# Row scatters of a routed two-expert layer: three supertiles at each end leave at once

## The chip, the cores and the metric

The kernel runs on one core of a Trainium2 chip. The metric is device time in microseconds of one execution. A core has five engines that run side by side and wait for each other by semaphores: TensorE (PE, with its weight loads as PEld), VectorE (DVE), ScalarE (ACT), GpSimd (POOL) and SyncE (SP). Each has its own instruction stream, which it executes in order. Transfers are issued by SyncE (plain ones here) and by GpSimd (indirect ones), and run on 16 shared DMA engines.

## The reference

The input x has 32 sequences of 256 tokens of 128 numbers, 8192 tokens in all. Two residual steps follow each other, both with a layer norm whose scale and shift come from a small conditioning matrix:

```python
h = _layernorm(x) * (1 + ca) + sa
x = x + ga * attn(h)       # g, a = sigmoid(linear(h)); v = linear(h)
                           # s_t = a_t * s_{t-1} + (1 - a_t) * v_t along the sequence; s * g
h = _layernorm(x) * (1 + cb) + sb
x = x + gb * ffn(h)

# ffn: 8 experts, each token goes to its best two
logits = x_flat @ gate_w.T + gate_b
probs = softmax(logits)
topk_vals, topk_idx = top_k(probs, 2)
h = relu(x_flat @ w1[e] + b1[e])     # 128 -> 512
y = h @ w2[e] + b2[e]                # 512 -> 128
out = sum over the two experts of topk_val * y
```

All arithmetic is float32; the up-projection is computed with the operands split into a leading part and a rest.

## The kernel before, in words

**The front.** Tokens are cut into 16 supertiles of 512 (`ST`; `T` = 4 tiles of 128). Each goes through four steps: the first norm (`a_norm`), the gates and the scan (`a_mix`), the residual and second norm (`a_res`), and the routing (`a_route`). `HEAD` and the list `steps` run them as a pipeline: step t works on several supertiles at once, each at another stage.

**The rows on their way out.** `a_route` writes, for each of a supertile's 4 tiles and 2 choices, 128 rows of 130 numbers (the normed token, its weight and its place in the output) into a tile `rw`, of which there are three, and computes the row numbers `pi` at which they belong in an expert-sorted region `reg` in HBM. The eight indirect transfers (L447) that scatter them are not issued there: L453 puts them on a list, `sending`. The function `drip` takes a few from it: one or two after each step of the front (L725), and one, later two, in each turn of the expert part (L648). Each then waits, by a dependence added by hand (L465), for a given ScalarE instruction of that step, so that it leaves at that pace. `sent` keeps what was issued.

**The tables.** After some supertiles (`TAKE`) a table says which blocks of 256 rows of `reg` are complete, and of which expert they are. There are 71 blocks. The first table, after supertile 2, has 5; after supertile 12 the tables together have 45 (blocks 0 to 44); the last one, after supertile 15, has the other 26. A table's blocks wait in `held` and are moved to `blocks` when its supertile's eight scatters have been issued (L467 to L469).

**The expert part.** `b_step` runs one turn: it issues loads for up to `LOOK` blocks ahead (`b_load`, L538 and L544: the rows `xr`, 130 KB, and the expert's first weights `ww`, 514 KB), transposes one block (`b_in`, L551 to L554), does the up-projection of the one before (`b_up`, L566 to L574), and the down-projection of the one before that (`b_down`, L584 to L591), whose result `yt` goes by two indirect transfers (L593) to `yd` in HBM. There are eight `yt` tiles and five `ww` tiles. The load of a block waits, by hand again (L540), for the last 16 row scatters in `sent`, that is, for the last two supertiles' rows issued before it in the order of the program. `between` puts such turns between the steps of the front; after the last step (`alive = False`) the turns run alone. At the end `c_load` and `c_add` read both results of each token, add them and write the output.

**Who sets the order.** The order in which instructions are written is not the order in which they are built: a scheduler that models the engines' times orders each engine's stream, with the front at a higher priority (`AHEAD`). On GpSimd the row scatters (L447), the block outputs (L593) and the small copies into `rw` (L445) share one stream. A copy of the normed rows into `rw` (L402, ScalarE) has to wait until the scatters that read this tile three supertiles earlier have landed.

Of the kernel before, what the change touches and what calls it, by code (L numbers as in the profile page):

```python
# [16 lines left out]
WAIT = mybir.DependencyInfo(mybir.DependencyClass.Sync, mybir.DependencyReason.DATA)  # L17
# [7 lines left out]
T = 4  # L25
BLK = 256

TAKE = (2, 3, 4, 5, 6, 7, 8, 10, 12)
CUT = 9

HEAD = "n0|m0 n1|r0 m1 n2|R0 r1 m2 n3|R1 r2 m3 n4|R2 r3 m4 n5"

# [22 lines left out]
def adaln_moe(ctx: ExitStack, tc: tile.TileContext, x, Wg, bg, Wv, bv, Wd, bd,  # L55
# [7 lines left out]
    NS = N // ST  # L63
    BPS = ST // S
    JB = T // BPS
    K = 2
# [5 lines left out]
    of = out.rearrange("b s d -> (b s) d")  # L72
# [19 lines left out]
    rows = cp.tile([P, D], F32, name="rows")  # L92
# [38 lines left out]
    def full(s):  # L131
        return max(0, -((E * (BLK - 1) - K * (s + 1) * ST) // BLK))

    def touched(s):
        return (K * (s + 1) * ST + E * (BLK - 1)) // BLK


    CLS = [CUT] + list(range(TAKE[-1], NS))
    NC = len(CLS)
# [80 lines left out]
    def late_constants():  # L220
        nc.vector.tensor_copy(b2s[:, 0], b2r)
        nc.vector.tensor_tensor(b2s[:, 1], b2r, b2s[:, 0], op=ALU.subtract)
        for h in range(2):
            nc.sync.dma_start(b2w[h:h + 1].bitcast(F32), b2s[:, h].bitcast(F32))


        sT3 = cp.tile([P, 3, NB], F32, name="sT3")
        nc.vector.tensor_copy(sT3, sT.unsqueeze(1).to_broadcast([P, 3, NB]))
        pr = psa.tile([P, 512], F32, tag="pq", name="pr")
        nc.tensor.matmul(pr[:N3, :D], sT3.rearrange("p a b -> p (a b)"), wm[:, 5 * D:], start=True, stop=True)  # L230
        mr = cp.tile([N3, D], F32, name="mr")
        guarded(mr, pr[:N3, :D], [N3, D], 1.0, "gr")
        nc.vector.tensor_copy(mr3, mr)
        for i in (1, 2, 2):
            w = slice(i * NB, (i + 1) * NB)
            nc.vector.tensor_tensor(mr[w], mr[w], mr3[w], op=ALU.subtract)
            nc.vector.tensor_copy(mr3[w], mr[w])

        nc.vector.tensor_tensor(sel, ident[:N3, 0:NB], ident[:N3, NB:2 * NB], op=ALU.add)
        nc.vector.tensor_tensor(sel, sel, ident[:N3, 2 * NB:N3], op=ALU.add)  # L240

    def stage(e):
        w1s = bk.tile([P, H], F32, tag="hh", name=f"w1s{e}")
        nc.sync.dma_start(w1s, w1[e])
        wh = bk.tile([P, WW], F32, tag="ww", name=f"wh{e}", bufs=5)
        nc.scalar.activation(wh[:, :H].bitcast(F32R), w1s, AF.Copy)
        nc.gpsimd.tensor_tensor(wh[:, H:2 * H].bitcast(F32R), w1s, wh[:, :H], op=ALU.subtract)
        nc.gpsimd.tensor_copy(wh[:, O_B1:], cols[:, 3 + e * NH:3 + (e + 1) * NH])
        nc.sync.dma_start(wd[e], wh)
# [62 lines left out]
    def a_norm(s):  # L312
        g = LN1G.get(s, 0)
        if g:
            mv = wk.tile([P, g * T, 2], F32, tag=f"mva{g}", name=f"mva{s}")
            for i in range(g):
                stats(mv[:, i * T:(i + 1) * T], xa[:, s + i], f"a{s + i}")
            y, r = rsqrt(mv, f"a{s}", s)
            for i in range(g):
                ln1[s + i] = (y[:, i * T:(i + 1) * T], r[:, i * T:(i + 1) * T])  # L320
        y, r = ln1[s]
        xn = wk.tile([P, T, D], F32, tag="xn", name=f"xn{s}")
        for j in range(T):
            last = nc.scalar.activation(xn[:, j], xa[:, s, j], AF.Identity, scale=y[:, j], bias=r[:, j])  # L324
        return dict(s=s, xn=xn, last=last)
# [43 lines left out]
    def a_res(a):  # L369
        s, og = a["s"], a["og"]  # L370
        xt = xa[:, s]
        po = early(s, "pbx", f"po{s}")
        for j in range(T):
            nc.tensor.transpose(po[:, j * P:(j + 1) * P], og[:, j * P:(j + 1) * P], ident)
        xm = xt.rearrange("p t d -> p (t d)")
        nc.vector.tensor_tensor(xm, po, xm, op=ALU.add)
        mv = wk.tile([P, T, 2], F32, tag="mvb", name=f"mvb{s}")
        stats(mv, xt, f"b{s}")
        y, r = rsqrt(mv, f"b{s}", s)
        xn = wk.tile([P, T, D], F32, tag="xm", name=f"xm{s}")  # L380
        for j in range(T):
            a["last"] = nc.scalar.activation(xn[:, j], xt[:, j], AF.Identity, scale=y[:, j], bias=r[:, j])
        a["xn"] = xn

    def a_route(a, base):
        s, xn = a["s"], a["xn"]
# [64 lines left out]
            return w.ins  # L451

        sending.extend((s, send, j, k) for j in range(T) for k in range(K))  # L453
        return rk[:, T]


    sending = []
    sent = []
    held = []

    def drip(n, behind):
        for _ in range(min(n, len(sending))):
            s, send, j, k = sending.pop(0)
            w = send(j, k)
            tc.add_manual_dep(w, behind.ins.name, WAIT, reason="pace of the rows on their way out")  # L465
            sent.append(w)
            if not sending or sending[0][0] != s:  # L467
                while held and held[0][0] <= s:
                    blocks.extend(held.pop(0)[1])  # L469

    def table(i, counts, done, n, last):

# [49 lines left out]
    def fills(base):  # L522
        fi = wk.tile([1, E], I32, tag="fi", name="fi")
        nc.vector.tensor_copy(fi, base[0:1, :])
        for e in range(E):
            r = nc.sync.value_load(fi[0:1, e:e + 1], min_val=e * CAP, max_val=e * CAP + N)
            w = nc.sync.dma_start(reg[bass.ds(r, BLK)].rearrange("(t p) d -> p t d", p=P), pad)
            into_reg(w.ins, "fill")
# [97 lines left out]
    blocks = []  # L626
# [33 lines left out]
    def between():  # L660
        nonlocal slot
        slot += 1
        if slot % SKIP and len(blocks) - len(flow) > BACK:
            b_step()

    counts = []
    st = {}

    def late():

        for s in range(XE, NS):
            load_x(s)
        for e in range(E):
            nc.sync.dma_start(wr[:, e].rearrange("p (k o) -> p k o", o=D), w2[e].rearrange("(k p) o -> p k o", p=P))


    steps = [[("nmrR".index(w[0]), int(w[1:])) for w in part.split()] for part in HEAD.split("|")]
# [6 lines left out]
    for t, todo in enumerate(steps):  # L684
        def step3(s):
            nonlocal base, done
            with tc.high_priority(AHEAD[3] * (s >= EARLY)):
                base = a_route(st[s], base)
                if s in CLS:
                    b = cp.tile([P, E], F32, name=f"cnt{s}")  # L690
                    nc.vector.tensor_copy(b, base)
                    base = b
                    counts.append(b)
                nb = len(blocks) + sum(len(x) for _, x in held)
                if s in TAKE:
                    n = full(s) - nb
                    tb, done = table(s, counts[:1] * (s > CUT) + [base], done, n, False)
                    held.append((s, [(tb, q, []) for q in range(n)]))
                elif s == NS - 1:
                    n = touched(s) - nb  # L700
                    tb, done = table(NS, counts, done, n, True)
                    fills(base)
                    rest = [(tb, q, []) for q in range(n)]
                    held.append((s, rest))
                    z = 0
                    for c in CLS:
                        u = max(E, touched(c) - nb) if c == CUT else touched(c) - nb
                        rest[u - 1][2].extend(range(z, c + 1))
                        z = c + 1

        def step2(s):
            with tc.high_priority(AHEAD[2] * (s >= EARLY)):
                a_res(st[s])

        def step1(s):
            with tc.high_priority(AHEAD[1] * (s >= EARLY)):
                a_mix(st[s])

        def step0(s):
            with tc.high_priority(AHEAD[0] * (s >= EARLY)):  # L720
                st[s] = a_norm(s)

        for i, s in todo:
            (step0, step1, step2, step3)[i](s)
            drip(2 if t < len(steps) - NS or len(sending) > K * T else 1, st[s]["last"])  # L725
            between()
        if t == 0:
            for e in range(E):
                stage(e)
            late()  # L730
        if t == LATE:
            late_constants()
# [32 lines left out]
```

## Time and profile before

The median of three runs is 546.61 us (538.9 to 547.15). The profiled execution took 472.67 us, 470.9 of it the span between the first and the last instruction.

| | busy us | share of the span | instructions |
|---|---|---|---|
| PE | 411.4 | 87% | 2810 |
| PEld | 346.6 | 74% | 2810 |
| DVE | 283.6 | 60% | 1511 |
| ACT | 291.4 | 62% | 726 |
| POOL | 291.9 | 62% | 322 |

The mean granted clock of TensorE was 0.908. 91.52 MB were moved, at 194 GB/s on average.

A group of the profile reads: line, engine, operation, what is written from what, count, then busy time and the mean of one in ns, then the idle time of the engine just before these instructions and what ended most of it. "issue" is time in which the engine waited for nothing that the profile shows. A line of the timeline reads: start, length (both in us), engine, line, operation, and in brackets the idle time before it with what released it. SPq lines are transfers that SyncE issues; their length is that of the issue.

### The profile page before, as it was taken

How to read it: one execution, taken by the hardware profiler on the slowest of the kernel's cores; microseconds unless marked ns; L12 is line 12 of the kernel's file. 1: busy time of each engine (PE TensorE's matmuls, PEld its weight loads, DVE VectorE, ACT ScalarE, POOL GpSimd, SP SyncE). 2: the span in 40 equal slices, each digit the busy share in tenths (PEclk: the TensorE clock that was granted, in tenths of full speed). 3: DMA queues.
4: the chain of work that ended last, by engine and by line, in shares of the span. 5: the costliest groups of instructions: out<-in, count | busy, mean ns of one | idle time of the engine just before them, and what ended most of it. 6: DMA issues, size and time to landing. Idle time of an engine off the chain costs nothing.

```text
span 470.9 us, 11399 instructions
## 1 busy us (share of the span) xinstructions
PE 411.4 (87%) x2810; PEld 346.6 (74%) x2810; DVE 283.6 (60%) x1511; ACT 291.4 (62%) x726; POOL 291.9 (62%) x322
## 2 busy tenths in 40 slices
PE   4867767779999999998997999999949999899980
PEld 3324433458888888987886999999839999799970
DVE  6899999958987886883795535222102214344564
ACT  4777563777978778774665565555415566656540
POOL 3634655536777777777577777777773444534551
PEclk9895666679999999997999799999979999999996
DMA  6996211192727566455452766686269979999983
GB/s 198 335 314 248 91 34 40 42 284 92 239 77 253 149 191 184 146 156 162 154 163 62 228 199 192 187 275 173 89 183 285 282 210 278 303 327 314 279 244 113
DMA packets 81845, 91.52 MB, mean 194 GB/s; under 512 B 8577, under 2 KB 66408, under 8 KB 81782
## 3 DMA queue, kind: packets, MB, share of 16 engines
q1 hardware_dynamic: 73024, 73.84, 53.6%
q0 software_dynamic: 8704, 16.94, 10.4%
q8 instruction: 26, 0.43, 0.4%
q14 instruction: 37, 0.30, 0.2%
q10 hardware_dynamic: 54, 0.02, 0.0%
HBM read 64.24 MB, written 27.43 MB: 195 GB/s over the span
## 4 chain that ended last, share of the span: by engine, by line
PE 65%; DMA 10%; DVE 9%; ACT 7%; issue 4%; POOL 3%; SPq 2%; POOLq 0%; ACTq 0%; DVEq 0%
PE pby L587 26%; PE p L566 7%; PE pz L346 6%; PE p L567 6%; PE p L568 6%; PE pby L584 4%; PE pbx L551 3%; DMA reg<-rw,pi 2%; DMA yd<-yt,xr 2%; DMA xa<-in_L_attn_x_dram 2%; DMA ww<-wd 2%; DMA yk<-yd 2%; PE pl L397 2%; PE px L337 2%; POOL yd L593 1%
## 5 line engine op out<-in xcount | busy, mean ns | idle before, releaser
L593 POOL DMA_INDIRECT yd<-yt,xr x142 | 142.5, 1004 | 87.2 <-ACT yt L591 49.5
L447 POOL DMA_INDIRECT reg<-rw,pi x128 | 124.8, 975 | 52.5 <-issue 21.1
L587 PE MATMUL pby<-wr,hh 128*128 x1136 | 151.5, 286 | 0.0
L587 PEld LDWEIGHTS pby<-wr,hh 128*128 128x128 f32 x1136 | 137.2, 196 | 9.4 <-issue 0.9
L574 ACT ACTIVATE hh<-p,ww 128x256 f32<-128x256 f32 x231 | 97.6, 475 | 20.0 <-PE p L568 14.1
L591 ACT ACTIVATE yt<-pby,xr 128x128 f32<-128x128 f32 x142 | 44.9, 364 | 80.6 <-PE pby L587 80.6
L566 PE MATMUL p<-xs,ww 128*128 128x256 f32 x284 | 89.5, 317 | 4.6 <-DMA ww<-wd 4.0
L554 DVE TENSOR_TENSOR xs<-pbx,xs 128x256 fp32r<-128x256 f32 x71 | 29.9, 421 | 86.7 <-ACT xs L553 86.5
L568 PE MATMUL p<-xs,ww 128*128 128x256 f32 x284 | 81.6, 288 | 0.0
L567 PE MATMUL p<-xs,ww 128*128 128x256 f32 x284 | 81.5, 287 | 0.0
L346 PE MATMUL pz<-h,wT 128*128 128x512 f32 x96 | 58.8, 734 | 6.1 <-ACT tg L361 3.6
L566 PEld LDWEIGHTS p<-xs,ww 128*128 128x128 f32 x284 | 55.2, 195 | 6.3 <-issue 3.1
L567 PEld LDWEIGHTS p<-xs,ww 128*128 128x128 f32 x284 | 55.5, 195 | 0.7 <-issue 0.7
L568 PEld LDWEIGHTS p<-xs,ww 128*128 128x128 f32 x284 | 55.1, 194 | 0.2 <-issue 0.2
L346 PEld LDWEIGHTS pz<-h,wT 128*128 128x128 f32 x96 | 19.7, 233 | 21.6 <-issue 9.4
L551 PE MATMUL pbx<-ident,xr 128*128 128x128 f32 x142 | 28.8, 286 | 6.0 <-DMA xr<-reg 6.0
L572 DVE TENSOR_SCALAR hh<-p,ww 128x256 f32<-128x256 f32 x53 | 25.4, 480 | 12.4 <-ACT hh L574 10.3
L553 ACT ACTIVATE xs<-pbx 128x256 fp32r<-128x256 f32 x71 | 27.5, 387 | 7.4 <-PE pbx L551 7.4
L324 ACT ACTIVATE xn<-xa,nra,nya 128x128 f32<-128x128 f32 x64 | 26.4, 488 | 8.0 <-DVE nra L307 8.0
L618 DVE TENSOR_TENSOR ot<-yk 128x512 f32<-128x512 f32 (+1 forms) x17 | 11.3, 663 | 32.7 <-DMA yk<-yd 17.7
L584 PE MATMUL pby<-b2w,ones_r 2*128 x71 | 27.2, 383 | 2.3 <-ACT yt L591 2.0
L402 ACT ACTIVATE rw<-pb 128x1024 f32<-128x1024 f32 x16 | 16.3, 1022 | 18.4 <-issue 6.2
(181 smaller groups left out, 594.7 us busy)
## 6 DMA issues: line engine op xcount, KB each, us to landing
ww<-wd SPq DMA_DIRECT2D x71, 514.0 KB
xr<-reg SPq DMA_DIRECT2D x71, 130.0 KB
yk<-yd SPq DMA_DIRECT2D x30, 256.0 KB
wd<-wh SPq DMA_DIRECT2D x8, 514.0 KB
xa<-in_L_attn_x_dram SPq DMA_DIRECT2D x16, 256.0 KB
out_dram<-ot SPq DMA_DIRECT2D x15, 256.0 KB
yd<-yt,xr POOLq DMA_INDIRECT x142
w1s<-in_L_ffn_w_dram SPq DMA_DIRECT2D x8, 256.0 KB
```

Source lines behind the costliest of these rows:

```text
L346: nc.tensor.matmul(z, wT[:, i], h1, start=True, stop=True)
L447: w = nc.gpsimd.indirect_dma_start(out=reg, out_offset=bass.IndirectOffsetOnAxis(ap=pi[:, j * K + k:j * K + k + 1], axis=0), in_=rw[:, j, ...
L551: nc.tensor.transpose(px[:, j * P:(j + 1) * P], xr[:, j, 0:D], ident)
L554: nc.vector.tensor_tensor(xs[:, 1], px, xs[:, 0], op=ALU.subtract)
L566: nc.tensor.matmul(z, hi, xs[:, 0], start=True, stop=False)
L567: nc.tensor.matmul(z, hi, xs[:, 1], start=False, stop=False)
L568: nc.tensor.matmul(z, lo, xs[:, 0], start=False, stop=True)
L574: w = nc.scalar.activation(hh[:, k], p1[:, k - k0], AF.Relu, bias=bias)
L584: nc.tensor.matmul(py.rearrange("p (j d) -> p j d", d=D), ones_r, b2t, start=True, stop=False)
L587: nc.tensor.matmul(py[:, j * D:(j + 1) * D], hh[:, k, j * P:(j + 1) * P], we[:, k * D:(k + 1) * D], start=False, stop=(j == NJ - 1 and k = ...
L591: nc.scalar.activation(yt[:, j], py[:, j * D:(j + 1) * D], AF.Copy, scale=xr[:, j, D:D + 1])
L593: w = nc.gpsimd.indirect_dma_start(out=yd, out_offset=bass.IndirectOffsetOnAxis(ap=xr[:, j, D + 1:D + 2].bitcast(I32), axis=0), in_=yt[:, ...
```

## The change

Supertiles outside a range `PACED` = (3, 13), that is 0, 1, 2 and 13, 14, 15, issue their eight scatters at the end of `a_route`, together with all that is still on the list, and without the wait for a ScalarE instruction. Those of supertiles 3 to 12 stay on the list. The release of a table's blocks becomes a function, which is called after each scatter and also once at the end of the routing step. In the step loop the condition on the first three steps is dropped.

```diff
+PACED = (3, 13)
...
         sending.extend((s, send, j, k) for j in range(T) for k in range(K))
+        if not PACED[0] <= s < PACED[1]:
+            drip(len(sending), None)
         return rk[:, T]
...
+    def release():
+        while held and not (sending and sending[0][0] <= held[0][0]):
+            blocks.extend(held.pop(0)[1])
 
     def drip(n, behind):
         for _ in range(min(n, len(sending))):
             s, send, j, k = sending.pop(0)
             w = send(j, k)
-            tc.add_manual_dep(w, behind.ins.name, WAIT, reason="pace of the rows on their way out")
+            if behind:
+                tc.add_manual_dep(w, behind.ins.name, WAIT, reason="pace of the rows on their way out")
             sent.append(w)
-            if not sending or sending[0][0] != s:
-                while held and held[0][0] <= s:
-                    blocks.extend(held.pop(0)[1])
+            release()
...
                         rest[u - 1][2].extend(range(z, c + 1))
                         z = c + 1
+                release()
...
-            drip(2 if t < len(steps) - NS or len(sending) > K * T else 1, st[s]["last"])
+            drip(2 if len(sending) > K * T else 1, st[s]["last"])
```

## The prediction

> **What bounds the kernel now.** I read the slices first, then the two GpSimd groups, then the timeline where the slices dip, then busy times by stretch. The rows of the slices are tenths of busy time in slices of 11.8 us.
>
> ```profile
> PE   4867767779999999998997999999949999899980
> POOL 3634655536777777777577777777773444534551
> PEclk9895666679999999997999799999979999999996
> ...
> L593 POOL DMA_INDIRECT yd<-yt,xr x142 | 142.5, 1004 | 87.2 <-ACT yt L591 49.5
> L447 POOL DMA_INDIRECT reg<-rw,pi x128 | 124.8, 975 | 52.5 <-issue 21.1
> ```
>
> TensorE is full from 106 us on, except for two slices (247 to 259 us, a 7; 341 to 353 us, a 4). GpSimd at 7 looks free but is not: each scatter takes 0.98 us and then shows 0.30 us of "issue", so a scatter costs 1.27 us of the queue, and tenths of 7 to 8 mean a queue that never rests. The timeline of GpSimd shows starts 1.27 us apart almost without a break from 111 to 353 us. So two engines are full at once between 111 and 345 us. The hole comes from the second:
>
> ```profile
> 327.14 0.37 SPq L538 DMA_DIRECT2D xr<-reg  x1
> 331.13 0.38 PE L551 MATMUL pbx<-ident,xr 128*128 128x128 f32 x2
> ...
> 338.71 0.99 POOL L593 DMA_INDIRECT yd<-yt,xr  x1 [0.30 <-DMA reg<-rw,pi]
> ...
> 341.29 0.97 POOL L447 DMA_INDIRECT reg<-rw,pi  x1 [0.30 <-DMA yd<-yt,xr]
> 342.56 0.95 POOL L447 DMA_INDIRECT reg<-rw,pi  x1 [0.30 <-DMA yd<-yt,xr]
> 343.82 0.98 POOL L593 DMA_INDIRECT yd<-yt,xr  x1 [0.30 <-DMA reg<-rw,pi]
> 344.96 0.37 SPq L538 DMA_DIRECT2D xr<-reg  x1
> 345.64 0.35 SPq L544 DMA_DIRECT2D ww<-wd  x1
> 347.20 0.48 PE L551 MATMUL pbx<-ident,xr 128*128 128x128 f32 x1 [4.10 <-DMA xr<-reg]
> ```
>
> The last row scatter (L447, supertile 15) starts at 342.56; block 45 of 71, the first of the last table, waits for it and is loaded at 344.96, 2.40 us later. Bias matmuls of successive blocks (L584) start 3.93 us apart before and after: 328.93, 332.86 ... 362.50, 366.44. Blocks 42 and 47 stand at 332.86 and 362.50; five intervals are 19.65 us, so the hole costs 10.0 us. The stretches, with columns window, length, busy PE, PEld, DVE, ACT, POOL, clock, DMA share, GB/s:
>
> ```profile
> 60.00:82.00 22.00, 15.92 (x48) 8.20 (x46) 20.90 (x142) 11.77 (x26) 12.71 (x14) 0.66 0.12 40
> 82.00:98.00 16.00, 10.83 (x41) 6.91 (x41) 14.70 (x133) 11.13 (x24) 8.31 (x9) 0.61 0.31 82
> 98.00:106.00 8.00, 6.94 (x39) 5.77 (x40) 4.18 (x33) 6.23 (x15) 1.92 (x2) 0.79 0.97 319
> ...
> 335.00:355.00 20.00, 12.48 (x80) 11.15 (x79) 1.82 (x4) 5.15 (x14) 14.48 (x15) 0.83 0.50 152
> ```
>
> Before 98 us VectorE is the full engine (35.6 of 38 us from 60 to 98) and TensorE idles 12.3 us between 60 and 106.
>
> **What the Trainium skill says.** "DMA: Bandwidth & Descriptors", section "Anatomy of one DMA — SWDGE (gpsimd) path", puts the fixed cost of such a DMA at about 2.0 us, mostly the receipt of the write, and has semaphore waits done by the issuing sequencer before dispatch. The trace agrees: a row scatter lands 2.27 us after its start (chain of waits, 337.45), while the next starts after 1.27. So eight scatters in a row cost 8 x 1.27 = 10.2 us of queue, and a waiting scatter holds all behind it. The same page, "Issuing engines are not separate DMA queues", says that all issuers share the 16 DMA engines; here that hardly matters: GpSimd's queue takes 10.4% of them. "TensorE: Matmul & The Clock Gate", section "What's actually happening", has the array slow until it has been kept busy; the clock is 0.66 from 60 to 82 us and 1.00 from 106 to 180.
>
> **The change part by part.** The sum is made against the profiled execution: 470.9 us of span plus 1.8 around it, 472.67. The median of the runs shown, 546.61, is 73.9 us longer; no view shows where. If it is TensorE that runs slower there, GpSimd has slack and the hole shrinks. So I carry both: the profile as it stands, and a run paced by TensorE.
>
> *Start.* The first table's five blocks wait for the 24 row scatters of supertiles 0 to 2. Now the last of these starts at 89.86 and block 0 is loaded at 92.46. In the changed program they stand back to back after one copy. Supertile 0 ends as before; the 16 others start at 60.0, so the last starts at 60.0 + 15 x 1.265 = 79.0, and block 0's load leaves at about 81.6, 11 us earlier. On TensorE the block now stands ahead of a transpose of the front that ran at 82.87, and its up-projection ahead of supertile 5's; its weights landed 4.7 us after issue (93.65 to 98.3), so they come at about 87.5. Front work waits some 5 us there, ScalarE and VectorE with it. Three blocks (11.8 us) are done before the front's step at 103.81; at most 6.3 us of idle lie after 82, and a warmer clock gives perhaps 2 more. TensorE thus gains 6 to 8 us; the front gets 4 to 6 us later. GpSimd gains less: by 110.7 us it has done 33 of these DMAs, afterwards some 36, since it must wait for block 0's output around 100 us: 3 x 1.27 = 4 us (0 to 7).
>
> *Middle.* Supertiles 3 to 12 keep their pace: the edit of the count in the step loop touches the first three steps alone, in which no row is ready yet, so it costs 0. Three extra blocks lie ahead of each front step. The rings of three rw tiles stay tied to GpSimd: ScalarE already waits there (4.7 us at 252). Cost: 0 in the sum, -3 to +4 us for the range.
>
> *End.* Supertiles 13, 14 and 15 lose eight waits each. This costs no engine anything; it moves queue positions. In the built order the outputs of blocks 35 to 40, 12 scatters, go behind supertile 15's rows instead of ahead: -12 x 1.28 = -15.4 us. Last row scatter: 342.56 - 15.4 = 327.2, minus the 4 us of the start = 323.2; the waiting load follows 2.40 later, at 325.6.
>
> But SyncE's loads wait for the last 16 scatters *written before them in the program*. Before, supertile 15's were written a few at a time between the loads of blocks 40 to 45, so only block 45 needed the last. Now all are written at once, and in the built order it is block 40's load that waits on all eight queue lanes. Blocks 40 to 44 belong to an older table and need none of these rows. So 31 blocks, not 26, come after the wait. The old rest took 470.9 - 344.96 = 125.9 us; five blocks more make 125.9 + 19.65 = 145.6. The end is 325.6 + 145.6 = 471.2: **+0.3 us**. The break-even is a load at 325.3. The stall itself moves from block 45 to block 40 and does not get smaller: TensorE, three blocks ahead, runs dry near 315. What is late next is again supertile 15's last scatter, with four block outputs (31 to 34) ahead of it. Block outputs now wait up to 20-odd us on GpSimd; the ring of eight yt tiles (eight blocks, 31 us) covers that, and if it did not, ScalarE would stall within the hole.
>
> *If TensorE paces the run*, GpSimd's 1.27 us a scatter hides behind blocks of about 5 us (3.93 x 546.61/472.67 = 4.5, more where only TensorE slows), neither hole opens, and what remains is the start: -6 to -8 us.
>
> Between 0 and -7 I take -4 us: **543 us**.
>
> **The rivals.**
> *The wait goes away (about 531).* If GpSimd keeps up, supertile 15's rows leave when its indices are ready (pi at 291.85) plus 10.2 us and no load is late: 10.0 us of hole and 6 to 8 of start, 16 to 18 us, 529 to 531. For: dense 1.27 us spacing can vanish when TensorE is slower. Against: 12 scatters saved out of 210, and outputs 31 to 34 stand ahead; and if GpSimd keeps up because TensorE is slow, there was less hole to win.
> *Slower (about 558).* Mechanism: the waiting load moved to block 40 with a queue that is not ahead. The bursts of supertiles 13 and 14 push the last two rows of supertile 12 behind eight others (10.2 us); rw of supertile 15 needs that buffer, ScalarE waits for it in order, and the block outputs ahead of supertile 15's rows come late. Every microsecond of the load after 325.3 is one lost; from 336 on it is over 2%. For: this wait already took 4.7 us at 252 and 1.4 at 290. Against: by the count of the queue that row moves by five DMAs (6 us) less the 4 of the start. With 12 us of it: 558.
> *It does not do what it says.* The waits are gone from the built program, so no.
> *Nothing measurable.* The profile case alone: 547.
>
> **How the numbers follow.** Forecast, the stall moves and little changes (539 to 549): 0.62. The wait goes: 0.24. Slower: 0.14. Two per cent (10.9 us) is about what a measurement of this kernel can tell from no change; its three runs lie 8 us apart. Of the 0.24 some 0.18 is beyond 535.7, of the 0.14 some 0.11 beyond 557.5; the forecast's own edges add 0.01 each. Range: 531 to 555, which takes in the first rival's upper half and the start of the second; it leaves out about 0.2.
>
> **What would show it.** In the profile after: block 0 loaded near 82 us and TensorE fuller from 84 to 106; row scatters of supertiles 13 to 15 in three groups of eight, 1.27 us apart; the gap in row loads ahead of block 40, ending near 326; a PE slice that dips near 315 to 335; 31 blocks at 3.93 us after it. Wrong would be: a load of block 40 before 315 or after 336; no gap at all; waits of ScalarE on row scatters beyond 10 us; a TensorE that idles as long before 106 us as now. The total goes wrong if the 74 us between profile and median sit elsewhere than in TensorE, since then their share in each stage is unknown.

## The result and the profile after

The changed kernel took 562.1 us (median of 4, 559.12 to 565.02) against 544.62 for the kernel before: a ratio of 1.036 (95% interval 1.024 to 1.047), slower. 543 us was forecast, with a range of 531 to 555.

One and the same program ran, by whole series of runs, at one of two levels, and one chip gave both: the kernel before at 474.5 to 475.7 us (here called the lower level, three series and the profile before) or at 543.0 to 546.8 us (the upper level, five series, among them the timed comparison and the profile after), so that only a comparison within a level tells what the change does.

The slices and the two GpSimd groups of the kernel after (span 560.9 us, so slices of 14.0 us):

```profile
PE   5658606987689799886978974775769999989991
POOL 4537650366376666646566565736343454534452
PEclk9976657979689899899889796878689999999996
...
L600 POOL DMA_INDIRECT yd<-yt,xr x142 | 142.1, 1001 | 140.9 <-ACT yt L598 110.3
L449 POOL DMA_INDIRECT reg<-rw,pi x128 | 123.8, 967 | 90.8 <-issue 35.4
```

GpSimd is no longer a full queue: it waits 110.3 us for results of blocks, where it waited 49.5. Only from 420 us on is TensorE full for more than two slices on end. It dips at 56 to 84 us, where the 24 scatters of supertiles 0 to 2 leave, and from 322 to 420 us, where those of 13 to 15 leave. The stretches at the start, with columns window, length, busy PE, PEld, DVE, ACT, POOL, clock, DMA share, GB/s:

```profile
60.00:82.00 22.00, 8.27 (x24) 4.11 (x22) 9.09 (x71) 8.76 (x20) 15.57 (x17) 0.58 0.15 48
82.00:98.00 16.00, 10.28 (x41) 6.58 (x42) 15.12 (x104) 7.20 (x15) 0.00 (x0) 0.71 0.69 207
98.00:106.00 8.00, 8.00 (x55) 6.83 (x55) 7.57 (x62) 6.37 (x16) 0.85 (x1) 0.90 0.01 3
```

The scatters do leave back to back (17 GpSimd instructions in 22 us), and block 0 is loaded at 82.24 us. But VectorE, the full engine of this stretch, is busy for 9.09 us where it was 20.90. Its timeline shows how:

```profile
69.59 0.17 DVE L522 TENSOR_SCALAR g<-g 128x8 f32<-128x8 f32 x1 [0.42 <-DVE smt L516]
70.33 0.16 DVE L305 SCALAR_TENSOR_TENSOR nya<-nta,nya 128x4 f32<-128x4 f32 x1 [0.57 <-DVE g L522]
71.74 0.15 DVE L517 TENSOR_SCALAR tb<-smt 128x1 int32<-128x1 f32 x1 [1.25 <-DVE nya L305]
...
75.98 0.17 DVE L524 TENSOR_TENSOR done<-g,done 128x8 f32<-128x8 f32 x1 [1.88 <-remote]
```

Small operations of 0.15 us stand 0.4 to 1.9 us behind VectorE's own last instruction, or behind nothing that the profile can name ("remote"). The profile before has no such line between 66 and 84 us. The profile after is of the upper level and the profile before of the lower one, so these differences hold what the level does as well as what the change does; in the paced kernel at the upper level (e16 below) VectorE is busy for 18.33 us of this stretch.

The end, in the timeline of GpSimd, TensorE and SyncE's loads:

```profile
391.90 0.96 POOL L449 DMA_INDIRECT reg<-rw,pi  x1 [0.30 <-issue]
393.17 0.96 POOL L449 DMA_INDIRECT reg<-rw,pi  x1 [0.30 <-issue]
394.56 0.57 PE L591 MATMUL pby<-b2w,ones_r 2*128 x1 [7.58 <-issue]
398.77 0.00 SPq L545 DMA_DIRECT2D xr<-reg  x1
400.64 0.37 SPq L545 DMA_DIRECT2D xr<-reg  x1
```

The last row scatter starts at 393.17, block 40 is loaded at 398.77, and before 394.56 TensorE has stood for 7.6 us for no named reason.

### The profile page after: what moved, and what is told of

Read it like the earlier page. It is cut to its first block, busy times and chain, and to the rows that moved or that the text cites. A ratio compares the mean times of both kernels' runs of the same rounds, so it can differ in the third digit from the quotient of the medians.

```text
span 560.9 us, 11384 instructions
## 1 busy us (share of the span) xinstructions
PE 434.9 (78%) x2810; PEld 360.9 (64%) x2810; DVE 284.3 (51%) x1511; ACT 290.6 (52%) x726; POOL 290.4 (52%) x322
## 4 chain that ended last, share of the span: by engine, by line
PE 54%; DVE 16%; issue 9%; another core or an unknown queue 9%; DMA 5%; ACT 4%; SPq 2%; POOL 0%; ACTq 0%; POOLq 0%; DVEq 0%
PE pby L594 21%; PE p L573 5%; PE p L575 5%; PE p L574 5%; PE pz L348 5%; PE pby L591 3%; PE pbx L558 3%; DVE sta L282 2%; DMA xa<-in_L_attn_x_dram 2%; PE pl L399 2%; DVE hs L367 1%; DMA yk<-yd 1%; PE po L376 1%; PE ph L391 1%
## 5 line engine op out<-in xcount | busy, mean ns | idle before, releaser
L600 POOL DMA_INDIRECT yd<-yt,xr x142 | 142.1, 1001 | 140.9 <-ACT yt L598 110.3
L594 PE MATMUL pby<-wr,hh 128*128 x1136 | 162.5, 296 | 9.7 <-issue 9.7
L594 PEld LDWEIGHTS pby<-wr,hh 128*128 128x128 f32 x1136 | 145.7, 205 | 21.0 <-issue 12.6
L573 PE MATMUL p<-xs,ww 128*128 128x256 f32 x284 | 90.4, 322 | 5.0 <-ACT xs L560 2.1
L574 PE MATMUL p<-xs,ww 128*128 128x256 f32 x284 | 84.8, 299 | 0.4 <-issue 0.4
L575 PE MATMUL p<-xs,ww 128*128 128x256 f32 x284 | 83.4, 294 | 1.2 <-issue 1.1
L573 PEld LDWEIGHTS p<-xs,ww 128*128 128x128 f32 x284 | 57.5, 204 | 7.9 <-ACT xs L560 2.6
L574 PEld LDWEIGHTS p<-xs,ww 128*128 128x128 f32 x284 | 57.9, 204 | 2.2 <-issue 2.2
L575 PEld LDWEIGHTS p<-xs,ww 128*128 128x128 f32 x284 | 57.5, 203 | 0.6 <-issue 0.6
L591 PEld LDWEIGHTS pby<-b2w,ones_r 2*128 2x128 f32 x71 | 13.3, 187 | 37.1 <-issue 14.7
L384 ACT ACTIVATE xm<-xa,nrb,nyb 128x128 f32<-128x128 f32 x64 | 26.4, 485 | 15.1 <-DVE nrb L309 9.2
```

The source lines that it names most:

```text
L573: nc.tensor.matmul(z, hi, xs[:, 0], start=True, stop=False)
L574: nc.tensor.matmul(z, hi, xs[:, 1], start=False, stop=False)
L575: nc.tensor.matmul(z, lo, xs[:, 0], start=False, stop=True)
L591: nc.tensor.matmul(py.rearrange("p (j d) -> p j d", d=D), ones_r, b2t, start=True, stop=False)
L594: nc.tensor.matmul(py[:, j * D:(j + 1) * D], hh[:, k, j * P:(j + 1) * P], we[:, k * D:(k + 1) * D], start=False, stop=(j == NJ - 1 and k = ...
L600: w = nc.gpsimd.indirect_dma_start(out=yd, out_offset=bass.IndirectOffsetOnAxis(ap=xr[:, j, D + 1:D + 2].bitcast(I32), axis=0), in_=yt[:, ...
```

## Experiments

All edits are to the changed kernel; `PACED = (a, b)` names the supertiles that keep their pace, so (0, 16) paces all of them.

**Each end alone, and none (lower level).** 

```diff
-PACED = (3, 13)
+PACED = (0, 16)   # e1; e2: (3, 16); e3: (0, 13)
```

> The changed source with the range set to (0, 16): all scatters keep their pace, which gives the streams of the kernel before on every engine. Both theories: ratio 1.00 to the kernel before. What it is for: a second profile of the kernel before. If the 74 us between its profiled execution and its timed runs come from execution to execution, this profile has a span near 540 and shows in which stage they lie; theory 'end' expects its hole at the last table (block 45) to be smaller than 10 us there, theory 'start' expects its front to end some 50 to 70 us later than at 292 us.

> Range (3, 16): only supertiles 0 to 2 leave at once, 13 to 15 stay paced. Theory 'end' (the 17.5 us come from the loads of blocks 40 to 44, which now wait for supertile 15): ratio 0.98 to 1.00. Theory 'start' (24 scatters without a pause hold up VectorE and ScalarE in the front's first 100 us, and everything after is later): ratio 1.03 to 1.04, with pi of supertile 3 near 104 us.

> Range (0, 13): only supertiles 13 to 15 leave at once. Theory 'end': ratio 1.03 to 1.04, and a gap in row loads ahead of block 40 that is wider than the one ahead of block 45 in the kernel before. Theory 'start': 0.99 to 1.01.

Measured: paced 1.005 (1.003 to 1.008), first three unpaced 0.9985 (0.996 to 1.002), last three unpaced 1.000 (0.998 to 1.003). Theory 'start' had 1.03 to 1.04 for the second, theory 'end' the same for the third: neither end alone costs anything here. All this fell on the lower level. e1 has the instruction streams of the kernel before on every engine, so half a per cent is what a comparison may be off. With the front alone unpaced, TensorE reaches block 30 at 269.1 us (before: 284.9), but block 34 only at 300.3 (301.4): nearly all of the lead of 16 us is lost between. The timeline of this kernel (GpSimd and ScalarE) shows where:

```profile
284.66 0.95 POOL L449 DMA_INDIRECT reg<-rw,pi  x1 [0.30 <-issue]
285.92 0.96 POOL L449 DMA_INDIRECT reg<-rw,pi  x1 [0.30 <-issue]
288.54 1.02 ACT L404 ACTIVATE rw<-pb 128x1024 f32<-128x1024 f32 x1 [13.98 <-DMA reg<-rw,pi]
```

ScalarE waits 13.98 us for a row buffer; it comes free when the last of supertile 12's paced rows, started at 285.92 behind three of supertile 13, has landed. The front ran ahead of the rows, and the three buffers took the lead away.

**The change itself once more, the waits of the loads, and no pacing at all (lower level).** e4 and e6 let a load wait by hand only for rows of its own table's supertiles:

```diff
-        for x in sent[-2 * K * T:]:
+        for _, x in [y for y in sent if y[0] <= upto][-3 * K * T:]:
```

> The changed kernel, but the load of a block waits for the last 24 row scatters of the supertiles up to that of its own table, instead of the last 16 issued before it in the program; blocks 40 to 44 then need nothing of supertiles 13 to 15. Theory 'end': 0.99 to 1.00 (the loss of 17.5 us goes, since only block 45 waits for supertile 15). Theory 'start': 1.03 to 1.04 as the change.

> The changed kernel once more, beside the kernel before on one chip. In the comparison of the record it took 562.1 us against 544.6, a ratio of 1.036. Theory A (the end: the loads of blocks 40 to 44 wait for the last supertile's rows and TensorE stands there): the cost belongs to the program and comes back wherever it runs, ratio 1.02 to 1.04, load of block 40 more than 5 us after the last row scatter's predecessor of before, a gap of TensorE of 10 us or more between blocks 36 and 41. Theory B (the small waits that lengthen everywhere in the slower comparison, VectorE waiting for itself between 60 and 80 us and the front ending 18 us later): where the kernel before takes about 474 us the ratio is 0.99 to 1.01 and VectorE is busy for over 15 of the 22 us between 60 and 82.

> All scatters paced as in the kernel before; alone changed is which rows a block's load waits for: the last 24 of the supertiles of its own table, instead of the last 16 handed to the queue. It belongs with the run of the changed kernel with the same edit, which was slower than the kernel before by 1.4%. If the edit itself costs (loads that start earlier meet the row scatters and the fetches of weights), it is slower here too, ratio 1.01 to 1.02. If the edit is neutral alone and the cost lay in the bursts at both ends, ratio 0.995 to 1.005.

> No supertile is paced: all 16 send their eight scatters at once, 128 scatters in 16 bursts, where the change bursts six. The dose of whatever a burst costs is 16/6. Theory A: block loads are ordered behind bursts, so the front's rows leave sooner and the block outputs later; ratio about that of the changed kernel, within 1%. Theory B: VectorE and ScalarE wait for small things during every burst; ratio over that of the changed kernel by 16/6 of its excess, so 1.05 to 1.10 if the excess is 0.03, and the front's end (last copy of rows by the activation engine) is later by 20 us or more.

Measured: e4 1.014 (1.008 to 1.020), e5 (the change as it is) 1.017 (1.012 to 1.023), e6 0.995 (0.991 to 0.999), e7 (`PACED = (0, 0)`) 0.963 (0.957 to 0.968). e4 settled nothing: block 40 was still loaded at 331.57, 2.4 us after the last row scatter (329.18). A load evidently also waits, without being told by hand, for the last write into `reg`; e8 below takes that wait away too, and there the load leaves first. For e7 both theories had expected a cost; it was a gain of 3.7%.

The change costs at the lower level too, by half as much. Its timeline there:

```profile
286.96 0.96 POOL L449 DMA_INDIRECT reg<-rw,pi  x1 [0.30 <-DMA reg<-rw,pi]
289.68 1.02 ACT L404 ACTIVATE rw<-pb 128x1024 f32<-128x1024 f32 x1 [11.90 <-DMA reg<-rw,pi]
291.27 0.57 PE L591 MATMUL pby<-b2w,ones_r 2*128 x1 [9.05 <-ACT yt L598]
...
315.26 0.66 PE L558 MATMUL pbx<-ident,xr 128*128 128x128 f32 x2 [6.36 <-DMA xr<-reg]
...
325.13 0.96 POOL L449 DMA_INDIRECT reg<-rw,pi  x1 [0.30 <-DMA reg<-rw,pi]
327.79 0.38 SPq L545 DMA_DIRECT2D xr<-reg  x1
```

At 286.96 starts the eighth scatter of supertile 13. In the built order its eight stand together, ahead of the last two of supertile 12. Supertile 15's copy into `rw` waits for the buffer that these eight hold until they have landed, 11.90 us, and TensorE stands 9.05 us behind ScalarE. Before 315.26 it stands 6.36 us for the rows of block 38, loaded at 309.18, after the eight fills (padding rows for `reg`) that SyncE issues once supertile 15 is routed (299 to 308 us; block 38 was loaded at 303.8 in the profile before). And block 40's load leaves at 327.79, behind supertile 15's scatters, which no block before 45 needs.

With no pace anywhere nothing overtakes. The slices of e7 (458.7 us, 11.5 us each):

```profile
PE   4756866499999999999999999995899999899980
POOL 4544767137777777777777877777777654345451
```

TensorE is full from 92 us on but for one dip (310 to 333 us). There block 44, loaded at 320.20, waits for the last row scatter (317.64); the expectation of e11 below calls it block 41. 128 scatters in bursts hurt no engine here.

**Taking away the two waits (upper level).** e8 frees the loads of the rows of later supertiles (each supertile's scatters form a group of their own; `upto` is the supertile of the block's table); e9 has four `rw` and `pi` buffers, the last two lines below and the same for `pi`; e10 both; e11 is e8 with no pacing.

```diff
+        if upto < NS - 1:
+            for s in range(upto + 1, NS):
+                tc.declare_no_dep(w.ins, group=f"scat{s}", reason="rows of later tables")
-        for x in sent[-2 * K * T:]:
...
+        for s, x in sent:
+            if s <= upto:
...
-        rw = wk.tile([P, T, K, RW], F32, tag="rw", name=f"rw{s}", bufs=3)
+        rw = wk.tile([P, T, K, RW], F32, tag="rw", name=f"rw{s}", bufs=4)
```

> The changed kernel, but a block's load waits for the row scatters of its own table's supertiles alone; the wait for rows of later supertiles is taken away (each row group is declared apart, so the load of block 40 no longer stands behind supertile 15). The changed kernel itself took 482.6 against 475.7 (1.017). Theory A (loads of blocks that need none of the last rows wait for them): load of block 40 leaves before 318 instead of 327.8, TensorE's stand of 6.4 us at 309 goes, the total falls by 6 us or more, ratio 0.99 to 1.005. Theory C (ScalarE waits 11.9 us for a row buffer at 278 to 290, since the burst of supertile 13 overtook the last rows of supertile 12): that wait stays, the total falls by less than 4 us, ratio 1.01 to 1.02.

> The changed kernel with four buffers instead of three for the rows and their indices; nothing else. It takes away what ScalarE waits for at 278 to 290. Theory C: the 11.9 us wait of ScalarE and TensorE's stand of 9 us behind it go, the last supertile's rows are ready 10 us earlier and leave earlier, total down by 8 us or more, ratio 0.99 to 1.00. Theory A: the wait goes too, but the load of block 40 still stands behind the last row scatter, so the total falls by less than 4 us, ratio 1.01 to 1.02.

> Both edits on the changed kernel: a load waits for its own rows alone, and four row buffers. If the two waits are all that the change lost at the end, what remains is its gain at the start (TensorE 13 to 16 us ahead by block 30): ratio 0.965 to 0.98, no stand of TensorE over 5 us after 100. If a third cause exists (the spacing of 1.27 us on GpSimd's queue), ratio 0.985 to 1.00, with a stand at the first block of the last table.

> All 16 supertiles unpaced, and a load waits for its own rows alone. All unpaced took 0.963 of the kernel before, with one stand of 6.6 us at 316 where block 41 waited. Theory A: the stand moves to block 45 and shrinks or goes; ratio 0.945 to 0.96. If the stand is set by GpSimd's queue (last row scatter at 317.6), not by which block waits: ratio 0.96 to 0.965.

Measured against the kernel before, 543.0 in this series: e8 1.021 (1.012 to 1.030), e9 1.023 (1.015 to 1.031), e10 1.011 (1.001 to 1.020), e11 1.093 (1.083 to 1.104). The level was the upper one, so the times of day in the expectations do not apply; the ratios do. In e8 block 40 is loaded at 388.41, ahead of the last row scatter (391.26), in e9 the last eight scatters start at 368.7 instead of 384.3. Each edit alone leaves over half of the 3.6%, and its interval overlaps that of the change (1.024 to 1.047); both together leave 1.0%, with intervals apart. But e10 was expected at 0.965 to 0.98 if the two waits were all that the change lost, and at 0.985 to 1.00 if a third cause was the spacing on GpSimd's queue. It is above both, so at this level something else costs. What stands in its trace, and what no run took away, are the eight fills on SyncE's queue, ahead of block 38:

```profile
368.83 15.61 SPq L535 DMA_DIRECT2D reg<-pad  x8
386.89 0.01 SPq L546 DMA_DIRECT2D xr<-reg  x1
```

No theory had expected e11: what was 3.7% faster at the lower level without freed loads is 9.3% slower at the upper with them. e8 and e11 differ in the pace alone and ran in one series: 554.9 us against 593.0. Its slices (590.3 us), with the share by engine of the chain that ended last:

```profile
PE   5766538797592939597949678864599999979991
DVE  6999559554370716464537255322121221335354
...
PE 51%; DVE 18%; another core or an unknown queue 15%; issue 8%; DMA 3%; ACT 2%; SPq 1%; POOL 0%; ACTq 0%; DVEq 0%; POOLq 0%
```

TensorE now goes up and down with the bursts, and 23% of the chain is time that the profile can't put to anything on the core. One burst, 265.5 to 274.7 us, in the timeline:

```profile
273.04 0.16 DVE L305 SCALAR_TENSOR_TENSOR nyb<-ntb,nyb 128x4 f32<-128x4 f32 x1
274.75 0.28 PE L580 MATMUL p<-xs,ww 128*128 128x256 f32 x1 [0.44 <-issue]
279.82 1.02 ACT L395 ACTIVATE hT<-ph,sb,cb 128x256 f32<-128x256 f32 x2 [9.18 <-remote]
281.67 0.42 DVE L566 TENSOR_TENSOR xs<-pbx,xs 128x256 fp32r<-128x256 f32 x1 [8.47 <-ACT xs L565]
```

ScalarE needs a tile that TensorE had finished at 271.4 and starts 8.4 us later; ScalarE and VectorE stand until 5 and 7 us after the start of the last of the eight (274.70), and TensorE creeps.

**Is it the density of row scatters?** I took, for every 0.1 us from 100 us to 30 us before the last row scatter, the number of row scatters that started within the last 5.2 us (four follow each other at 1.27 us), and whether TensorE, VectorE and ScalarE were busy at that moment. Shares PE/DVE/ACT, and the time spent at four or more:

```
                                  one            two            three          four           time at 4+
lower  kernel before          .94/.61/.68    .97/.67/.71    .99/.63/.66   1.00/.82/.86     18 us
lower  e5, changed kernel     .99/.62/.83    .99/.79/.70    .96/.75/.78    .69/.54/.61     22 us
lower  e7, none paced        1.00/.81/.72   1.00/.85/.76   1.00/.89/.71   1.00/.66/.84     67 us
upper  e16, all paced         .94/.62/.66    .86/.49/.48    .57/.22/.34    .51/.09/.17     13 us
upper  changed kernel         .91/.76/.67    .87/.49/.53    .67/.25/.38    .41/.18/.14     21 us
upper  e18, rear unpaced      .95/.76/.70    .90/.46/.56    .59/.28/.35    .39/.01/.09     18 us
upper  e11, none paced        .66/.51/.54    .70/.28/.38    .64/.35/.22    .46/.21/.13     70 us
```

At the lower level the number makes no difference where no wait for a buffer falls into a burst; e5's drop at four is the 9.05 us of TensorE behind ScalarE shown above. At the upper one, with four behind them, VectorE and ScalarE all but stop, in every kernel, paced or not. Block outputs, the other indirect transfers of this queue, count too: in e16, with two row scatters in the 5.2 us, VectorE and ScalarE are busy for .71 and .68 when no block output is among them and for .34 and .32 when two are; TensorE stays at .83 and .84. With both kinds counted, the paced kernel too spends 88 us at four or more (.76/.26/.28, against .85/.56/.61 at three).

This is a correlation in each profile: engines that stand for another reason would also let GpSimd work off its queue. That the density is the cause rests on e8 against e11 and on the next runs, in which the range of the pace alone is changed. Such an edit also changes the order in which the queues were built; one program seen at both levels, below, holds that order fixed.

**The paced kernel and each end at the upper level.** e12 to e14 are the programs of e1 to e3, e15 is e10 with all paced. They fell on the lower level and repeat it.

> The instruction streams of the kernel before, engine by engine, for a profile at the level at which it is timed in this call. Ratio 1.00. Theory D (dense row scatters make the other engines stand, at the level of about 544 us only): at that level the paced kernel shows TensorE busy for over 0.8 where three row scatters left within 5.2 us, with less time spent at four or more than the changed kernel's 20 us, and its front ends 15 us or more earlier than the changed kernel's (last copy of rows at 366.9). At the level of 474 us no difference by density.

> The first three supertiles unpaced, the rest as before. At the level of 474 us: ratio 1.00 again. At the level of 544 us: theory D gives the burst of 24 scatters its own loss (front later by some 15 us, made up in part by the earlier first blocks), ratio 1.005 to 1.02; if the loss on record came from the end alone, ratio 0.99 to 1.00.

> The last three supertiles unpaced, the rest as before. At the level of 474 us: ratio 1.00 again. At the level of 544 us: if the loss came from the end (loads of blocks 36 to 40 behind the rows of supertiles 13 to 15, and stalls during three bursts), ratio 1.015 to 1.035; if from the start, 0.99 to 1.005.

> All paced, with loads that wait for their own rows alone and four row buffers. If these waits cost the kernel before as well, ratio 0.98 to 0.99; if block 45's wait for the last row scatter stays the bound, since GpSimd's queue is as long as it was, ratio 0.995 to 1.005.

Measured: 0.9985 (0.995 to 1.002), 0.996 (0.992 to 1.000), 1.001 (0.998 to 1.004) and 0.9955 (0.993 to 0.998). Freed loads and a fourth buffer give the paced kernel nothing beyond what two copies of one program differ by; its block 45 waits for the last row scatter as it did.

> The streams of the kernel before, for a profile. Ratio 1.00. At the level of about 544 us theory D expects TensorE busy for 0.8 or more with one scatter in the last 5.2 us and for 0.5 to 0.7 with three or four, as in the unpaced kernels at that level, but with less of the time at four than the 20 us of the changed kernel, and the last copy of rows before 352. At the level of 475 us: no difference by density, as before.

> The first three supertiles unpaced, the rest paced. Where the kernel before takes about 545 us: theory D expects the indices of supertile 3 near 104 instead of 91, the last copy of rows by 355 to 367 instead of 347, and a ratio of 1.005 to 1.02; if the start costs nothing, indices of supertile 3 near 97, the last copy of rows by 347 and a ratio of 0.98 to 1.00. Where the kernel before takes 475 us: ratio 0.995 to 1.00, as twice before.

> The last three supertiles unpaced, the rest as before. Where the kernel before takes about 544 us: if the end costs by itself (three bursts of eight in which the other engines stand, and the loads of blocks 36 to 40 behind their rows), ratio 1.02 to 1.035; if the loss needs both ends (an earlier start leads GpSimd's queue into the bursts with more outputs ahead), 1.00 to 1.015. Where the kernel before takes 475 us: 1.00, as twice before.

These three met the upper level. Paced: 1.001 (0.998 to 1.005). First three unpaced: 1.004 (1.0005 to 1.007). Last three unpaced: 1.015 (1.002 to 1.029). The start costs a little less than theory D had it: supertile 3's indices at 106 us, as the theory says, but the last copy of rows at 353.4 and the ratio both just under its ranges. The rear falls between its two ranges, and its interval takes in both. The two sum to 1.9%, the whole change has 3.6%; the intervals do not tell whether the ends add up or make each other worse.

The start shows most plainly what a burst does at the upper level. From 60 to 82 us, columns as above: first three unpaced at the lower level (e2), the same program at the upper (e17), all paced at the upper (e16).

```profile
60.00:82.00 22.00, 15.66 (x49) 8.36 (x47) 21.11 (x146) 12.59 (x26) 16.18 (x17) 0.66 0.15 49
60.00:82.00 22.00, 8.12 (x24) 4.20 (x24) 10.34 (x82) 8.76 (x20) 15.16 (x18) 0.58 0.14 45
60.00:82.00 22.00, 14.11 (x34) 6.50 (x34) 18.33 (x134) 10.65 (x23) 13.32 (x14) 0.63 0.11 37
```

With the same burst VectorE is busy for 21.11 us at the lower level and for 10.34 at the upper; at the upper, without it, for 18.33. It takes both, the level and the burst.

The profiles of the paced kernel (e16, first fence; an execution of 551.2 us, over the 544.6 of its series, so the comparison rather understates the change) and of the changed kernel (second) in the three stretches in which the changed one sends supertiles 13, 14 and 15, columns as above:

```profile
333.00:345.00 12.00, 9.90 (x59) 9.40 (x60) 3.85 (x23) 5.59 (x16) 4.71 (x5) 0.72 0.48 142
355.00:367.00 12.00, 10.62 (x81) 9.84 (x79) 1.70 (x4) 4.62 (x14) 7.43 (x8) 0.95 0.57 151
384.00:396.00 12.00, 8.90 (x60) 7.96 (x58) 1.81 (x4) 4.31 (x12) 7.31 (x9) 0.86 0.49 145
```

```profile
333.00:345.00 12.00, 2.86 (x14) 2.46 (x13) 2.14 (x11) 1.50 (x3) 8.47 (x9) 0.73 0.20 63
355.00:367.00 12.00, 6.74 (x36) 5.23 (x35) 0.66 (x2) 2.41 (x6) 7.88 (x9) 0.67 0.36 106
384.00:396.00 12.00, 4.25 (x28) 3.61 (x27) 0.00 (x0) 0.63 (x2) 8.86 (x11) 0.74 0.51 150
```

The paced kernel executes 200 matmuls there, the changed one 78: 122 fewer. By the same counts the changed kernel is 17 behind at 300 us (1291 to 1308) and falls back by another 114 between 300 and 420 us (543 to 657). The three bursts hold all of that. With the two waits taken away (e10) the count between 300 and 420 us is 610. At the lower level (e5) two of the same bursts leave TensorE alone:

```profile
296.00:308.00 12.00, 12.00 (x97) 11.16 (x95) 3.70 (x15) 6.75 (x19) 9.40 (x11) 1.00 0.74 182
316.00:328.00 12.00, 11.38 (x77) 10.44 (x77) 1.81 (x4) 5.07 (x14) 8.96 (x10) 0.87 0.33 99
```

Within the bursts of the changed kernel, how much is density and how much the two waits, is told only by these sums: 67 of the 114 matmuls come back without the waits, and the ratio goes from 1.036 to 1.011. What the start, the density and the fills have in the rest was not separated.

## Why the prediction was wrong

**The step that failed** is the sentence under *End*: taking the waits of supertiles 13 to 15 away "costs no engine anything; it moves queue positions". It costs in two ways. The burst of supertile 13 holds the buffer that the last copy of rows needs: ScalarE waits 11.90 us for it and TensorE 9.05 behind it (e5, 1.017 at the lower level). And at the upper level, at which the kernel was timed, TensorE does 122 matmuls fewer in the 36 us of the three bursts (1.036), where the two waits are one part and engines that stand for no named reason another. The forecast took its stalls from a profile in which a scatter costs GpSimd's queue and nobody else.

**The level.** "If TensorE paces the run", worth -6 to -8, was my reading of the 74 us between profile and median. The profile of the paced kernel at the upper level (e16, span 549.5) gives TensorE 439.1 us busy, 27.7 more than before, of a span 78.6 us longer. The other 51 us are TensorE idle, and VectorE, ScalarE and GpSimd are busy within 3 us for as long as before, so they too stand idle longer. Nor do the row scatters' own transfers get longer. Their queue in the kernel before (span 470.9) and in the kernel after (560.9):

```profile
q0 software_dynamic: 8704, 16.94, 10.4%
q0 software_dynamic: 8704, 16.94, 8.8%
```

Both shares are 49 us. So it is not TensorE that paces the run, and the -6 to -8 us do not come: the start alone costs 0.4% there (e17). The prediction had named this, the 74 us lying elsewhere than in TensorE, as what would make the total wrong. One part came out, though not for its reason: with GpSimd no longer full, the hole at block 45 is small there (bias matmuls of blocks 45 and 46 at 422.6 and 431.0 us, 4.5 more than a block's 3.93).

*Start.* At the lower level the mechanism was right: block 0's load at 83.35 (81.6 forecast), TensorE 9 us ahead at block 5 (127.2 to 136.3), above the 6 to 8. The price was set too low: supertile 3's indices come 11 us later (97.7 to 86.3), not 4 to 6. At the upper level TensorE is 15 us ahead at block 5 (137.3 to 152.6), but the front is 14 later at supertile 3's indices (104.1 to 90.6 us) and 20 later at the last copy of rows (366.9 to 346.9), and the lead is gone by block 30 (349.2 to 339.9).

*Middle, 0.* Wrong in what it hides: TensorE gains some 13 us by block 30 at the lower level (272.3 to 284.9), and loses nearly all of it in ScalarE's wait of 11.90 us. The sum had nothing for such a wait, the range up to 4 us, after waits of 1.4 and 4.7 in the profile before.

*End, +0.3.* At the lower level the mechanism was right and two terms were too small. The waiting block is 40, as said; its load leaves at 327.79 where I had 325.6 (+2.2); from there to the end it takes 480.9 - 327.8 = 153.1 us where I had 145.6 (+7.5). The sum, +0.3 + 2.2 + 7.5 = +10.0, is the difference of the spans, 480.9 - 470.9. Of the 7.5, 2.8 lie in the first five blocks after the load (32.0 us against 29.2), and 4.3 between blocks 50 and 60 (46.4 us against 42.1); but e12, with the streams of the kernel before, takes 45.2 there, so some 3 us are the spread of single executions. The ratio of medians, 1.017, makes it 8 us.

**The rivals.** *Slower (558)* named, as one mechanism, rows of supertile 12 pushed behind bursts, a ScalarE wait beyond 10 us, and a load of block 40 later than 325.3. All three are in the trace at the lower level (e5), and taking the two waits away (e10, upper level) takes away most of the loss. At the upper level no wait of ScalarE for row scatters beyond 10 us is named: the longest before a copy of rows is 8.6 us, put to "issue". The rival had 0.14, because I counted queue positions (six us against four) instead of following which buffer the last copy of rows would get: the one that supertile 13's burst was holding. Its size at the lower level is 8 us, not 12; at the upper one the standing of the engines comes on top. *The wait goes* is what happened with no pacing at all at the lower level (457.9, a gain of 17.8 us against 475.7, where I had 16 to 18). That the change could not get there because ten paced supertiles stood between the unpaced ones is my reading; no run shows it by itself.

**The Trainium skill.** "SBUF — State Buffer", section "Who interferes with whom", has DMA never contend with a compute engine, and leaves GpSimd only a port shared with VectorE to hold others up. The lower level agrees (e7, four scatters in a row, TensorE at 1.00). At the upper one TensorE and ScalarE, which have no part in that port, fall to 0.51 and 0.17 (e16). The measurement decides: whatever the page leaves out, every engine can stand while these scatters leave. It need not be that memory; which resource it is stays open. The profile gives these waits to the engine itself, to "issue" or to "remote", and no run separated the scatters' bytes, their count or their landing. Why the level changes from one series to the next is open too. No version here was shown to be faster at both levels: the unpaced one (e7) gains 3.7% at the lower and was not run at the upper; the only unpaced kernel that met the upper level (e11) lost 9.3%.

## What to carry to other kernels

A pace put on transfers may be there for engines that never touch them: before taking it away, look in a profile of the same level as the timing for engines that stand still while many transfers leave. Where the median and the profiled execution lie much further apart than the effect that you forecast (74 us here, for a forecast of 4), the profile's waits need not be those of the timed run, and the first thing to get is a second profile of the unchanged kernel. And where only a part of a stream loses its pace, look at what the burst overtakes: the slow ones before it, and with them every ring of buffers and every load that waits for "whatever was sent last".

## What the runs showed of the hardware

- One program, with the same streams, at 475 or at 545 us, by whole series of runs, on the same chip; at the upper level TensorE's granted clock is 0.88 (e16) against 0.92 (e12), and most of the difference is idle time of all engines (51 of 78.6 us for TensorE). The scatters' packets take 49 us of the DMA engines' time at both.
- There, four indirect row scatters within 5.2 us leave VectorE 0.01 to 0.21 busy (four kernels) where one leaves it 0.51 to 0.76; block outputs on the same queue add to it (e16: 0.71 to 0.34). After the burst shown for e11 ScalarE and VectorE stand for some 5 and 7 us more. In the burst at the start (60 to 82 us) VectorE is busy for 10.34 us (e17) where the same program at the lower level has 21.11 (e2); in the changed kernel it needs 0.4 to 1.3 us to follow its own previous instruction.
- The waiting load leaves 2.66 us after the last row scatter's start in the changed kernel at the lower level and 5.6 us at the upper, but 2.45 us at the upper in the paced kernel (408.99 to 411.44).
